# Layer 2's finishing of a graph network: the projection issued in pieces, layer norm in steps out of PSUM, and two more PSUM slots

## The chip, the cores and the metric

The kernel runs on one core of one Trainium2 chip. The metric is device time in microseconds (us). The core's engines each have a queue of their own that is worked through in order: PE (TensorE, matmuls), DVE (VectorE), ACT (ScalarE), POOL (GpSimd, which here only issues gathers) and SP (SyncE, which issues the other DMAs). Engines wait for each other through semaphores.

## The reference

```python
def _rgcn_layer(x, src, dst, edge_type, w_rel, root, bias):
    seg = dst * NUM_REL + edge_type
    xs = x[src]
    sums = jax.ops.segment_sum(xs, seg, num_segments=N * NUM_REL)
    cnt = jax.ops.segment_sum(jnp.ones(seg.shape, x.dtype), seg, num_segments=N * NUM_REL)
    mean = (sums / jnp.maximum(cnt, 1.0)[:, None]).reshape(N, NUM_REL, -1)
    return jnp.einsum('nrd,rdo->no', mean, w_rel) + x @ root + bias
...
h = jax.nn.relu(_rgcn_layer(x, src, dst, edge_type, w_rel1, root1, b1))
out = _layernorm(x + _rgcn_layer(h, src, dst, edge_type, w_rel2, root2, b2))
```

There are 12,500 nodes with 128 features, 200,000 edges sorted by destination, and 10 relations. The relation of an edge is the argmax of ten of its attributes. All is float32.

## The kernel before, in words

**Tiles and windows.** Edges are taken 128 at a time (a tile). POOL gathers the 128 source rows of a tile into a slot of `g` (`gathered`, L684; the pool has six buffers of eight slots, so 48 tiles can be gathered ahead). ACT multiplies each row with one over its count (`scaled`, L690). DVE builds a 0/1 matrix `oh` that tells for each edge its relation and its place in a window of w nodes (`ones`, L698 and L701). PE multiplies the two into a PSUM slot `zp` of 10 x w columns (L895 in layer 1, L1217 in layer 2), and DVE adds that to the running sums `cc` in SBUF (`sum_into`, L725). `cc` is a ring of 1,024 nodes for each layer.

**Blocks.** When all edges of a block of 512 nodes are in `cc`, the block is finished: `projected` multiplies the ten relations' sums with their weights (ten matmuls into one PSUM tile `pf`, L673) and adds one last matmul (L675), and the block's part of the ring is cleared on ACT (`cleared`, L656). Layer 1 also computes that part of layer 2's sums whose sources are known already, projects it (`second`, L808) and stores it transposed in DRAM as `T2`, bias and root term included.

**Layer 2** (`layer_2`, L1103) takes the tiles of which layer 1 could do nothing (166) and the edges left over, which `brought_together` and `listed` compress into 799 tiles. The fewer edges a row keeps, the wider is the window of a tile: w goes from 14 up to 46, in bunches of three tiles, then two, and from w = 26 on one tile to a bunch. The last 115 tiles have w = 46, which is 460 columns. The order of the instructions is written out by hand. For bunch p it records: `ones` for bunch p + 3; the gathers, scalings and matmuls of bunch p; `sum_into` of bunch p - 2; then the steps of a finished block that are due. `zp` has three PSUM buffers (`ps_y`, L952). The table that `ones` compares with is kept in the first 480 columns of a PSUM tile of three banks, `mask` (name "go", L958 and L1029 to L1031); its other two banks are only used while the list is made.

**Finishing in layer 2** (`finish`, L1153). A class `Later` holds steps with a due time, counted in tiles i. At i all eleven matmuls of the projection are recorded in one go, the last of them an identity matmul that adds the stored part `fT` (from `T2`). Then: `turn` at i + 6 (ACT copies `pf` to SBUF as `a`, L1164; PE transposes it, L1167), clearing at i + 8 and i + 12, and `norm` at i + 10 (`normed`, L627: DVE adds x from `xb`, L634; takes the moments, L637 and L638; ACT takes the square root, L640; DVE the reciprocal, L641, and four scalings, L644). Where the ring is about to be written again, `free_until(k)` is a latest time `by` for turning and clearing. With 128-node blocks at the end, layer 2 has 26 blocks, k = 0 to 25.

Of the kernel before, what the change touches and what calls it, by code (L numbers as in the profile page):

```python
# [9 lines left out]
F32 = mybir.dt.float32  # L10
BF16 = mybir.dt.bfloat16
I32 = mybir.dt.int32
AF = mybir.ActivationFunctionType
ALU = mybir.AluOpType
# [6 lines left out]
P = 128  # L21
NREL = 10
# [18 lines left out]
YB = 512  # L41
RN = 2 * YB
# [13 lines left out]
def rgcn_resnorm_kernel(ctx: ExitStack, tc: tile.TileContext, x, src, dst, attr, w_rel1, root1, b1,  # L56
# [498 lines left out]
    def block(k):  # L555
        n0 = nodes[-1][k]
        n = (nodes[-1] + [N])[k + 1] - n0
        return n0, n, [(t, min(P, n - t * P)) for t in range(-(-n // P))]
# [14 lines left out]
    def rows_in(k):  # L573

        last = "e" if k == len(nodes[-1]) - 1 else ""
        xb = fin.tile([P, len(block(k)[2]) if last else 4, C], F32, name="xb" + last)
        rows_dma(xb, x, k, False)
        return xb
# [72 lines left out]
    def cleared(l, k, h):  # L651

        n0, n, _ = block(k)
        o = n0 % RN
        H = NREL // 2
        nc.scalar.activation(cc[:, l, h * H:(h + 1) * H, o:o + n], zero[:, None, :n].to_broadcast([P, H, n]), AF.Copy)  # L656
# [6 lines left out]
        nc.vector.tensor_tensor(s, s, e, op=ALU.add)  # L663
        nc.vector.memset(e, 0.0)

    def projected(k, l, last, po=None, more=True):

        n0, n, _ = block(k)
        o = n0 % RN
        if po is None:  # L670
            po = ps_f.tile([P, YB], F32, name="pf")
        for r in range(NREL if more else 0):
            nc.tensor.matmul(po[:, :n], wsb[l][:, r, :], cc[:, l, r, o:o + n], start=(r == 0), stop=False)  # L673
        w, f = last
        nc.tensor.matmul(po[:, :n], w, f[:, :n], start=not more, stop=True)  # L675
        return po

    def stored(hb, b, k):
# [86 lines left out]
    def layer_1():  # L765
# [7 lines left out]
        def finish(k, t):  # L773

            todo.run(END)
            if k not in fTs:
                xbs[k] = rows_in(k)
                fTs[k] = features_in(k, 0, xbs[k])
            u = QB if t < NT else 0
            folded(ALL, k, WN)  # L780
            po = [projected(k, 0, (rsb[0], fTs[k]))]
            both = starts[k + 1] > bounds(T0)[0] if k + 1 < NBLK else True
            reused = starts[k] + RN < N
            assert not reused or t + 7 * u <= (starts[k] + RN - OFF - WN) // STEP

            def rows_out(_):
                a = po.pop()
                a = fin_a.setdefault(k, shifted(a, k, 0))
                pr = ps_f.tile([P, 4, C], F32, name="pf")
                n0, n, subs = block(k)  # L790
                for i, h in subs:
                    nc.tensor.transpose(pr[:h, i, :], a[:, i * P:i * P + h], ident)
                po.append(pr)

            def rows_kept(_):
                pr = po.pop()
                hb = fin.tile([P, 4, C], F32, name="hb")
                for p, s in spans(k):
                    nc.scalar.activation(hb[:p, s], pr[:p, s], AF.Copy)
                rows_dma(hb, hD, k, True)  # L800
                if k <= K1:
                    first = 0 if k <= K0 else (k - K0) % 2
                    stored(hb, first, k)
                    if k < K1:
                        when = t + 8 * QB if k < K0 else first_seen[k] + 2 * QB
                        todo_late.append((when, lambda t: stored(hb, 1 - first, k)))

            def second(_):  # L808
                po.append(projected(k, 1, (rsb[1], fin_a.pop(k)), more=both))

            def second_kept(_):
                n0, n, _ = block(k)
                p2 = po.pop()
                t2 = fin.tile([P, YB], F32, name="v")
                nc.scalar.activation(t2[:, :n], p2[:, :n], AF.Identity, bias=bsb[1])  # L815
                nc.sync.dma_start(T2[:, n0:n0 + n], t2[:, :n])

            todo.at(t + u, rows_out)
            todo.at(t + 2 * u, rows_kept)
            if reused:  # L820
                todo.at(t + 2 * u, lambda t: cleared(0, k, 0))
                todo.at(t + 3 * u, lambda t: cleared(0, k, 1))
            todo.at(t + 3 * u, second)
            todo.at(t + 5 * u, second_kept)
            if both:
                todo.at(t + 6 * u, lambda t: cleared(1, k, 0))
                todo.at(t + 7 * u, lambda t: cleared(1, k, 1))
            if k + 1 < NBLK - 1:
                def fetch(t):
                    xbs[k + 1] = rows_in(k + 1)  # L830

                def turn(t):
                    n0, n, subs = block(k + 1)
                    pt = ps_f.tile([P, YB], F32, name="pf")
                    for i, h in subs:
                        nc.tensor.transpose(pt[:, i * P:i * P + h], xbs[k + 1][:h, i, :], ident[:h, :h])
                    po.append(pt)

                def turned_kept(t):
                    n0, n, subs = block(k + 1)  # L840
                    pt = po.pop()
                    fTs[k + 1] = fin.tile([P, 4 * P], F32, name="fT")
                    nc.scalar.activation(fTs[k + 1][:, :n], pt[:, :n], AF.Copy)
                todo.at(t + u, fetch)
                todo.at(t + 5 * u, turn)
                todo.at(t + 6 * u, turned_kept)
# [256 lines left out]
    def layer_2():  # L1103
# [30 lines left out]
        def free_until(k):  # L1134

            return next((i for i, hi in enumerate(highs) if hi > starts_2[k] + RN), len(order))
# [3 lines left out]

        todo, jobs = Later(), Later()
        done = 0
        xbs, fTs = {}, {}

        def fetched(k):
            if k < NB2 and k not in xbs:
                n0, n, subs = block(k)
                last = "e" if k == len(nodes[-1]) - 1 else ""
                xbs[k] = rows_in(k)
                fTs[k] = fin.tile([P, (len(subs) if last else 4) * P], F32, name="fT" + last)  # L1150
                nc.sync.dma_start(fTs[k][:, :n], T2[:, n0:n0 + n])

        def finish(k, i):  # L1153

            todo.run(END)
            fetched(k)
            u = 1 if i < len(order) else 0
            folded(TWO, k, WZ)
            n = block(k)[1]
            po = [projected(k, 1, (ident, fTs[k]))]  # L1160

            def turn(_):
                a = fin.tile([P, YB], F32, name="a")
                nc.scalar.activation(a[:, :n], po.pop()[:, :n], AF.Copy)  # L1164
                pr = ps_f.tile([P, 4, C], F32, name="pf")
                for b, h in block(k)[2]:
                    nc.tensor.transpose(pr[:h, b, :], a[:, b * P:b * P + h], ident)  # L1167
                po.append(pr)

            def norm(_):  # L1170
                normed(k, xbs[k], po.pop())
                if k + 1 < NB2 - 1:
                    fetched(k + 1)

            reused = starts_2[k] + RN < N
            by = free_until(k) if reused else END
            assert i < by
            todo.at(min(i + 6 * u, by), turn)
            if reused:
                todo.at(min(i + 8 * u, by), lambda i: cleared(1, k, 0))  # L1180
                todo.at(min(i + 12 * u, by), lambda i: cleared(1, k, 1))
            todo.at(i + 10 * u, norm)

        fetched(0)
        flag = None
# [2 lines left out]
        i = 0  # L1188
        jobs.job(0, brought_together(), QB)
        NB = len(bunches)  # L1190
        made = 0
        for p in range(-AH, NB + BE):
            if p + AH < NB:
# [7 lines left out]
            if p < NB:  # L1201
                second, t0, n, w = bunches[p]
                oh = ohs.pop(p)
                zp = zps[p] = ps_y.tile([P, YB], F32, name="zp")
                for j in range(n):
                    if made % GQ == 0:
                        g = gpool.tile([P, GQ * C], F32, name="g")
                    gs[p, j] = g, made % GQ
                    made += 1
                    idx = (idxB if second else idxE)[:, t0 + j:t0 + j + 1]  # L1210
                    gathered(g, gs[p, j][1], hD, idx, 1)
                for j in range(n):
                    scaled(*gs[p, j], (wB if second else wE)[:, t0 + j:t0 + j + 1])
                m = NREL * w
                for j in reversed(range(n)):
                    gt, b = gs.pop((p, j))
                    nc.tensor.matmul(zp[:, j * m:(j + 1) * m], gt[:, b * C:(b + 1) * C], oh[:, j * m:(j + 1) * m],  # L1217
                                     start=True, stop=True)
                i += n
# [199 lines left out]
```

## Time and profile before

| what | value |
|---|---|
| runs shown | 3320.06, 3318.46, 3319.7 us; median 3319.7 us |
| profiled execution, its own time | 3311.85 us |
| its span in the trace | 3309.8 us |
| busy: PE, DVE, ACT, POOL | 71%, 59%, 50%, 73% |
| gathers issued: layer 1, layer 2 | 166 + 1397, 166 + 799 |
| first and last gather of layer 2 start at | 1982.0 and 3208.2 us of the span |
| layer 2's last projection starts at | 3294.15 us |

An engine's busy share is an average over stages with different limits. In most of the span POOL issues one gather after the other; the last hundred microseconds have no gather any more. So the questions to the profile are how long POOL sets the pace, and what works on after its last gather.

### The profile page before, as it was taken

How to read it: one execution, taken by the hardware profiler on the slowest of the kernel's cores; microseconds unless marked ns; L12 is line 12 of the kernel's file. 1: busy time of each engine (PE TensorE's matmuls, PEld its weight loads, DVE VectorE, ACT ScalarE, POOL GpSimd, SP SyncE). 2: the span in 40 equal slices, each digit the busy share in tenths (PEclk: the TensorE clock that was granted, in tenths of full speed). 3: DMA queues.
4: the chain of work that ended last, by engine and by line, in shares of the span. 5: the costliest groups of instructions: out<-in, count | busy, mean ns of one | idle time of the engine just before them, and what ended most of it. 6: DMA issues, size and time to landing. Idle time of an engine off the chain costs nothing. (4 is left out here: it accounts for less than half of the span.)

```text
span 3309.8 us, 38851 instructions
## 1 busy us (share of the span) xinstructions
PE 2335.7 (71%) x10229; PEld 1650.2 (50%) x10229; DVE 1962.0 (59%) x4847; ACT 1670.3 (50%) x4283; POOL 2404.7 (73%) x2542
## 2 busy tenths in 40 slices
PE   3657777777778777777777871455656677778887
PEld 2445555555556555555655571344444445433333
DVE  7655656565646565555555543977644546567775
ACT  4336666666666666666666663134333434434232
POOL 7777777777777777777777757777777777777750
PEclk7769899988888898888898995567656667799998
DMA  7675444545444545454544332122222222222220
GB/s 229 184 204 178 132 150 131 158 124 157 127 153 128 154 128 158 122 159 120 155 117 123 113 113 66 50 71 78 64 62 63 72 62 72 62 73 81 72 61 28
DMA packets 257039, 376.78 MB, mean 114 GB/s; under 512 B 50066, under 2 KB 181315, under 8 KB 256812
## 3 DMA queue, kind: packets, MB, share of 16 engines
q0 software_dynamic: 103248, 257.39, 27.1%
q1 hardware_dynamic: 99763, 91.19, 8.7%
q10 hardware_dynamic: 53801, 25.62, 2.7%
q8 instruction: 87, 1.43, 0.2%
q14 instruction: 140, 1.15, 0.1%
HBM read 330.41 MB, written 56.39 MB: 117 GB/s over the span
## 5 line engine op out<-in xcount | busy, mean ns | idle before, releaser
L684 POOL DMA_INDIRECT g<-XH,idxE x1397 | 1321.1, 946 | 431.6 <-issue 405.7
L725 DVE TENSOR_TENSOR cc<-cc,zp 128x240 f32 (+15 forms) x2528 | 978.2, 387 | 1094.3 <-PE zp L895 542.7
L895 PE MATMUL zp<-oh,g 128*128 128x120 f32 x5920 | 911.4, 318 | 487.7 <-ACT g L690 389.9
L895 PEld LDWEIGHTS zp<-oh,g 128*128 128x128 f32 x5920 | 851.6, 227 | 584.2 <-ACT g L690 474.3
L684 POOL DMA_INDIRECT g<-hD,idxB x799 | 756.6, 947 | 244.4 <-issue 218.8
L690 ACT ACTIVATE g<-g,wE 128x128 f32<-128x128 f32 x1729 | 665.3, 394 | 510.5 <-DMA g<-XH,idxE 319.5
L1217 PE MATMUL zp<-oh,g 128*128 128x120 f32 (+16 forms) x1930 | 617.6, 472 | 422.5 <-ACT g L690 251.9
L1217 PEld LDWEIGHTS zp<-oh,g 128*128 128x128 f32 x1930 | 409.5, 263 | 624.1 <-ACT g L690 462.1
L673 PE MATMUL pf<-cc,w 128*128 128x512 f32 (+2 forms) x1600 | 665.2, 573 | 10.2 <-DVE cc L663 6.6
L690 ACT ACTIVATE g<-g,seenE 128x128 f32<-128x128 f32 x1397 | 543.8, 389 | 0.0
L690 ACT ACTIVATE g<-g,wB 128x128 f32<-128x128 f32 x799 | 283.6, 394 | 378.5 <-DMA g<-hD,idxB 344.8
L673 PEld LDWEIGHTS pf<-cc,w 128*128 128x128 f32 x1600 | 304.3, 203 | 332.5 <-issue 310.7
L656 ACT ACTIVATE cc<-zero 128x2560 f32<-128x2560 f32 (+2 forms) x144 | 318.3, 2220 | 2.3 <-DVE keyb L1065 1.2
L701 DVE TENSOR_TENSOR oh<-go,keyB 128x460 f32<-128x460 f32 (+11 forms) x481 | 274.0, 570 | 0.0
L698 DVE TENSOR_TENSOR oh<-bank,keyE 128x480 f32<-128x480 f32 x391 | 253.2, 648 | 0.0
L684 POOL DMA_INDIRECT g<-hD,idxE x166 | 166.7, 1004 | 76.3 <-issue 51.8
L684 POOL DMA_INDIRECT g<-in_x_dram,idxE x166 | 156.9, 945 | 51.6 <-issue 45.7
L1164 ACT ACTIVATE a<-pf 128x512 f32<-128x512 f32 (+3 forms) x26 | 14.8, 571 | 275.7 <-PE pf L675 275.7
L606 ACT ACTIVATE a<-pf,b 128x512 f32<-128x512 f32 (+2 forms) x28 | 17.6, 630 | 200.2 <-PE pf L675 200.2
L476 DVE TENSOR_TENSOR eqb<-bank,kh 128x1344 bf16<-128x1344 f32 (+2 forms) x65 | 100.4, 1548 | 0.4
L815 ACT ACTIVATE v<-pf,b 128x512 f32<-128x512 f32 (+2 forms) x28 | 17.7, 632 | 146.9 <-PE pf L675 131.8
L485 PE MATMUL pf<-eqb,identb 128*128 128x512 bf16 (+2 forms) x130 | 55.1, 424 | 10.9 <-DVE eqb L476 10.8
(185 smaller groups left out, 895.4 us busy)
## 6 DMA issues: line engine op xcount, KB each, us to landing
m<-in_edge_attr_dram SPq DMA_DIRECT2D x48, 672.0 KB
g<-XH,idxE POOLq DMA_INDIRECT x1397, 2.8
g<-hD,idxB POOLq DMA_INDIRECT x799, 2.5
XH<-in_x_dram ACTq DMA_DIRECT2D x24, 512.0 KB
XH<-zero ACTq DMA_DIRECT2D x24, 512.0 KB
xb<-in_x_dram SPq DMA_DIRECT2D x46, 256.0 KB
XH<-hb SPq DMA_DIRECT2D x35, 256.0 KB
hD<-hb SPq DMA_DIRECT2D x23, 256.0 KB
```

Source lines behind the costliest of these rows:

```text
L476: nc.vector.tensor_tensor(eq[:p], kpP[:p, None, :R].to_broadcast([p, DB, R]), fore, op=ALU.is_equal)
L485: nc.tensor.matmul(pc[:p], identb[:p, :p], eq[:p, k:k + 4, L:], start=(d + k == 1), stop=False)
L656: nc.scalar.activation(cc[:, l, h * H:(h + 1) * H, o:o + n], zero[:, None, :n].to_broadcast([P, H, n]), AF.Copy)
L673: nc.tensor.matmul(po[:, :n], wsb[l][:, r, :], cc[:, l, r, o:o + n], start=(r == 0), stop=False)
L684: nc.gpsimd.indirect_dma_start(out=g[:, j * C:(j + n) * C], out_offset=None, in_=table, in_offset=bass.IndirectOffsetOnAxis(ap=idx, axis=0))
L690: nc.scalar.activation(s, s, AF.Copy, scale=w)
L698: nc.vector.tensor_tensor(o.rearrange("p (t m) -> p t m", m=m), cols[:, None, :m].to_broadcast([P, n, m]), keys[:, :, None].to_broadcast([ ...
L701: nc.vector.tensor_tensor(o.rearrange("p (t r n) -> p t r n", r=NREL, n=w), cols[:, None, :, :w].to_broadcast([P, n, NREL, w]), keys[:, :, ...
L725: nc.vector.tensor_tensor(s, s, z, op=ALU.add)
L815: nc.scalar.activation(t2[:, :n], p2[:, :n], AF.Identity, bias=bsb[1])
L895: nc.tensor.matmul(zp[:, a + l * KW:a + (l + 1) * KW], g[:, (slot[j] + l) * C:(slot[j] + l + 1) * C], oh[:, j * KW:(j + 1) * KW], start=Tr ...
L1217: nc.tensor.matmul(zp[:, j * m:(j + 1) * m], gt[:, b * C:(b + 1) * C], oh[:, j * m:(j + 1) * m], start=True, stop=True)
```

## The change

It touches both layers. In layer 1, `second` adds x to the stored part: one more identity matmul, with the block's transposed features. In layer 2:

- the x rows are not loaded any more; `fT` alternates between two buffers, and the next block's is asked for when a block begins to finish
- the eleven matmuls are eleven steps, spread over `spread` tiles, where `spread` is at most 10 and at most `by - i - 3`
- `turn` comes at i + spread + 4, clearing at i + spread + 5 and i + spread + 8, none later than `by`
- layer norm reads the transposed block from PSUM, in four steps two tiles apart: `moments` (DVE), `deviation` (ACT), `factors` (DVE), `put` (ACT, four scalings with a bias)
- from the fourth bunch of compressed tiles on, two of every five `zp` slots are the other two banks of `mask`

```diff
-    def projected(k, l, last, po=None, more=True):
+    def projected(k, l, last, more=True):
...
-        w, f = last
-        nc.tensor.matmul(po[:, :n], w, f[:, :n], start=not more, stop=True)
+        for i, (w, f) in enumerate(last):
+            nc.tensor.matmul(po[:, :n], w, f[:, :n], start=not more and i == 0, stop=i == len(last) - 1)
...
-                po.append(projected(k, 1, (rsb[1], fin_a.pop(k)), more=both))
+                po.append(projected(k, 1, [(rsb[1], fin_a.pop(k)), (ident, fTs[k])], more=both))
...
-            po = [projected(k, 1, (ident, fTs[k]))]
+            live = i < len(order)
+            spread = max(0, min(10, by - i - 3)) if live else 0
+            u = 1 if live else 0
+            po = [ps_f.tile([P, YB], F32, name="pf")]
+            some = {}
+
+            def piece(r):
+                w, f = (ident, fTs[k][:, :n]) if r == NREL else (wsb[1][:, r, :], cc[:, 1, r, o:o + n])
+                nc.tensor.matmul(po[0][:, :n], w, f, start=r == 0, stop=r == NREL)
...
-            def norm(_):
-                normed(k, xbs[k], po.pop())
-                if k + 1 < NB2 - 1:
-                    fetched(k + 1)
...
+            def moments(_):
+                mv = some["mv"] = small.tile([P, 4, 2], F32, name="mv")
+                for t, h in subs:
+                    st = small.tile([P, nc.vector.BN_STATS_DIM], F32, name="st")
+                    nc.vector.bn_stats(st[:h], po[0][:h, t, :])
+                    nc.vector.bn_aggr(mv[:h, t, :], st[:h])
+            def deviation(_):
...
+                    nc.scalar.activation(some["rstd"][:p, s], some["mv"][:p, s, 1], AF.Sqrt, bias=eps[:p])
+            def factors(_):
...
+                    nc.vector.reciprocal(some["rstd"][:p, s], some["rstd"][:p, s])
+                    nc.vector.scalar_tensor_tensor(some["back"][:p, s], some["mv"][:p, s, 0], -1.0, some["rstd"][:p, s],
+                                                   op0=ALU.mult, op1=ALU.mult)
+            def put(_):
...
+                    nc.scalar.activation(out_rows[:h, t, :], pr[:h, t, :], AF.Identity, bias=some["back"][:h, t:t + 1],
+                                         scale=some["rstd"][:h, t:t + 1])
+                rows_dma(out_rows, out, k, True)
+            for r in range(NREL + 1):
+                todo.at(i + r * spread // NREL, lambda _, r=r: piece(r))
+            todo.at(i, lambda _: fetched(k + 1))
+            todo.at(min(i + (spread + 4) * u, by), turn)
             if reused:
-                todo.at(min(i + 8 * u, by), lambda i: cleared(1, k, 0))
-                todo.at(min(i + 12 * u, by), lambda i: cleared(1, k, 1))
-            todo.at(i + 10 * u, norm)
+                todo.at(min(i + (spread + 5) * u, by), lambda i: cleared(1, k, 0))
+                todo.at(min(i + (spread + 8) * u, by), lambda i: cleared(1, k, 1))
+            for j, step in enumerate((moments, deviation, factors, put)):
+                todo.at(i + (spread + 6 + 2 * j) * u, step)
...
+        FIRST = sum(not b[0] for b in bunches) + AH
...
-                zp = zps[p] = ps_y.tile([P, YB], F32, name="zp")
+                spare = (p - FIRST) % 5 if second and p >= FIRST else 0
+                if spare < 3:
+                    zp = zps[p] = ps_y.tile([P, YB], F32, name="zp")
+                else:
+                    zp = zps[p] = mask[:, (spare - 2) * YB:(spare - 1) * YB].bitcast(F32)
```

## The prediction, made before the change was run

> **What bounds the kernel now.** I read the stages first, then who waits at the end. POOL's own row for the compressed tiles of layer 2 (engine, op, tile: shortest/median/longest ns, first and last start):
>
> ```profile
> L684 POOL DMA_INDIRECT g<-hD,idxB x799: 940/944/1297, 2208.5 to 3208.2; - x200
> ```
>
> 799 gathers in 1000 us are one per 1.25 us without a break, so up to 3208 POOL sets the pace. But the span goes on to 3309.8: 101.6 us of work are behind. The waits of ACT after 2997 us (engine, line, releaser: us in all, times, longest) tell since when:
>
> ```profile
> ACT a L1164 <- PE pf L675: 141.2, 11, 20.2
> ...
> ACT g L690 <- DMA g<-hD,idxB: 16.4, 18, 1.9
> ```
>
> ACT hardly waits for a gather any more. It stands in front of a projection, 141 of 313 us. So from about 2960 on, tiles are ready before they are used, and the backlog grows. Who is the bound there? DVE's timeline of the block k = 20 (start, duration, work, idle before):
>
> ```profile
> 3173.41 0.62 DVE L725 TENSOR_TENSOR cc<-cc,zp 128x460 f32 x1
> 3173.95 0.63 DVE L701 TENSOR_TENSOR oh<-go,keyB 128x460 f32<-128x460 f32 x1
> 3181.87 0.63 DVE L725 TENSOR_TENSOR cc<-cc,zp 128x460 f32 x1 [7.29 <-PE zp L1217]
> 3182.42 0.63 DVE L701 TENSOR_TENSOR oh<-go,keyB 128x460 f32<-128x460 f32 x1
> 3182.97 0.62 DVE L725 TENSOR_TENSOR cc<-cc,zp 128x460 f32 x1
> ...
> 3190.03 0.68 DVE L634 TENSOR_TENSOR v<-pf,xb 128x512 f32<-128x512 f32 x1
> ...
> 3193.02 1.11 DVE L644 TENSOR_SCALAR o<-v,mv,rstd 128x128 f32<-128x128 f32 x4
> 3194.05 0.62 DVE L701 TENSOR_TENSOR oh<-go,keyB 128x460 f32<-128x460 f32 x1
> 3194.60 0.62 DVE L725 TENSOR_TENSOR cc<-cc,zp 128x460 f32 x1
> ```
>
> and PE's of the same block:
>
> ```profile
> 3171.35 8.85 PE L673 MATMUL pf<-cc,w 128*128 128x512 f32 x20
> 3180.04 1.02 PE L675 MATMUL pf<-fT,ident 128*128 128x512 f32 x2
> 3180.90 4.93 PE L1217 MATMUL zp<-oh,g 128*128 128x460 f32 x12
> ```
>
> A tile costs DVE a `sum_into` and a `ones`, from 3181.87 to 3182.97: 1.09 us. It costs PE two passes, 4.93/12 x 2 = 0.8 us (0.77 between starts). So DVE is the bound, but for the 7.3 to 7.9 us of a projection, and for the norm, 3190.03 to 3194.05 = 4.0 us. Check: 20 x 1.09 + 7.3 + 4.0 + 0.8 (folding) = 33.9, and from this projection to the next, at 3205.08, are 33.7. POOL needs 20 x 1.25 = 25. From the projection at 2959 to the one at 3269 nine blocks (k = 14 to 22: 25, 28, 25, 22, 20, 18, 20, 21, 14 tiles) take 310 us.
>
> **The change, part by part**
>
> *The two spare PSUM slots.* They lie in the tile whose first bank holds the table that `ones` reads. In the order of the changed kernel's built instructions, with what each waits for, the program takes that tile as one. The `ones` after a matmul into a spare slot waits for this matmul, and a matmul into a spare slot waits for the `ones` recorded just before it. In before no `ones` waits for PE. So in two of five bunches DVE and PE go one after the other: `ones` 0.63, then 0.14 until the matmul starts (a sum that ends at 3195.22 lets PE start at 3195.36), then a lone pair of passes 1.04 (PE at 3160.61). That is 1.81 us where DVE needs 1.09, so 1.44 us more for five tiles. At 290 columns (rows: `ones` 0.451, pair 0.76) the step is 1.35 against 0.74, 1.2 more for five. Before 2960 this hides under POOL: with 290 columns five tiles then cost 2 x 1.35 + 3 x 0.74 = 4.9 us, and POOL needs 6.25. Behind it nothing hides it, for DVE is the bound; queued behind the waiting `ones` is every sum. The nine blocks have 193 tiles. In each I take off 8: about six in which PE is the bound anyway (next part), two hidden under the norm's steps. That leaves 121 tiles, 24 groups of five at 1.35: **+33 us**. Bounds: 0, if the order's waits are always over in time, and 193/5 x 1.44 = 56.
>
> The Trainium skill, "PSUM — Partial Sum Buffer", section "PSUM bank collisions raise a hardware error", asks for a guard only between engines in one bank; the table and the spare slots are in different banks. By that rule the chip needs none of these waits, and the sum would lack the 33 us (first rival). They are in the program all the same.
>
> *The projection in pieces.* Same passes: 22 x 0.43 = 9.5 us of PE. The due times give the spread: `by - i - 3` is 4, 9, 7, 5, 1, 1, 4, 5, 4 for k = 14 to 22, so it never reaches 10 here. With a spread of 4, PE does 9.5 us and five tiles (3.9) in a row, 13.4 us, in which DVE wants 5.5 and a tile or two of lead. It loses 13.4 - 6.5 = 7, as now (7.3 to 7.9). Cover would need PE's slack of 1.09 - 0.77 = 0.3 us per tile, some 30 tiles. **-3 us** in all; bounds -10 and +8.
>
> *Norm.* DVE loses the addition and the scalings. It keeps the moments (3190.75 to 3192.44 in before: 1.7 us) and gets `factors`, two operations like L641 (0.18) with a gap, 0.45. So 2.15 for 4.0, nine times: **-17 us**. No row shows the statistics read PSUM; DVE's copies out of PSUM of this size (L1088, 266 ns) take what the statistics take from SBUF (269), so I take no difference. `put` costs ACT four scalings at 0.30 to 0.39, and ACT is idle for two thirds of a block. If its function needed another table, each block would pay two loads like the page's ACT_TABLE_LOAD (1283 ns), 0 to 2.6 us of ACT; only two such loads stand in the whole span, though square root and copy alternate 27 times, so 0.
>
> *Clearing.* Turning and both clears now fall together on `by`, three tiles behind the last piece. ACT copies and clears for 0.6 + 4.55 = 5.1 us and no tile is scaled meanwhile, while PE has three scaled tiles, 3 x 1.3 = 3.9 us. Before, the copy came earlier, and in two blocks DVE lost 1.3. Net about 1 per block: **+8 us** (0 to +18).
>
> *Start of the backlog.* At k = 14 POOL is still close: the first 4 us vanish in its slack: **-4**.
>
> *The rest.* Early in layer 2 POOL waits 2.0, 2.2 and 4.7 us, the last behind a projection of 10.6 us at 2144.3; in pieces, **-2** (0 to -4.7). Layer 1 gets 28 more identity matmuls (L675: 1.02 us for 512 columns, 0.39 for 128) beside a PE that POOL keeps waiting; only those of the last four small blocks stand on the path: **+1**. Of SP's DMAs, the x rows go; nobody waited for them but in the last blocks, where PE waits 3.4 us for `fT`. That wait goes, but the last blocks' chains (pieces, copy, transposes, moments, root, factors, `put`) still run one after the other, and `put` now stands ahead of the last tiles' scaling on ACT: 0 (-4 to +4).
>
> Sum: 33 - 3 - 17 + 8 - 4 - 2 + 1 = **+16**. A second way: I walked through k = 20 instruction by instruction with these durations, from the `ones` of its tile i. Last piece ends at 14.1; `ones` of i + 8 at 17.6 (before 16.7); ACT's clump holds `ones` of i + 10 until 21.6; moments 22.7 to 24.4; the next block's at 36.4, against 33.8 in before: +2.6. Nine such blocks less the 4 are +20. I take **+18**. On the profiled execution's own 3311.85 (span 3309.8 and 2 us around it) that is 3330; it lies 8 below the median of the runs shown, and I count from the median: 3319.7 + 18 = **3338**.
>
> **The rivals**
>
> *The spare slots' waits cost nothing* (0.20). If PE is always far enough ahead, the sum is 16 - 33 = -17 at most. My walk without these waits gives 33.25 for k = 20, -0.5 per block, since ACT's clump then shows in full: -5, with the -2 some **3312**. It decides if five tiles of 460 columns still take 5.45 us.
>
> *The pieces do remove DVE's stall* (0.08, the other side): 7.5 x 9 = 68 us less, **3252**. That needs PE to run the pieces while DVE sums, so a lead of six tiles; it has two, and at spread 1 (k = 18, 19) ten pieces stand in a row as now.
>
> *The clock falls* (0.10). PE's lines in the gather-bound stage:
>
> ```profile
> 2592.65 1.57 PE L1217 MATMUL zp<-oh,g 128*128 128x180 f32 x4 [1.26 <-ACT g L690]
> ...
> 2622.70 1.99 PE L1217 MATMUL zp<-oh,g 128*128 128x180 f32 x12
> 2624.53 0.60 PE L1167 MATMUL pf<-ident,a 128*128 128x128 f32 x4
> 2625.34 0.85 PE L1217 MATMUL zp<-oh,g 128*128 128x180 f32 x4 [0.22 <-DVE cc L725]
> ```
>
> The same four passes take 1.57 us with pauses of about 1 us and 0.85 behind a projection: the granted clock was halved. With more pauses in the backlog stage, the two lone pairs of each group of five could take 1.8 for 1.04: 24 x 1.5 = 36 more, **3374**. Against it: at 290 columns with pauses of 0.5 us (2949 to 2959) the granted clock was 1.00, and there PE streams less (0.5 of 1.25 us) than it would here (3.85 of 6.9). The Trainium skill, "TensorE: Matmul & The Clock Gate", "HAM oscillation", names only pauses over some 3.4 us as harmful; by it this rival has no chance, but the row above has half the clock at pauses of 1.3 us, so it keeps one.
>
> **How the numbers follow.** Forecast 0.60 (3338, own range 3322 to 3356 by the bounds), free waits 0.20, no stall 0.08, clock 0.10, else 0.02. A measurement tells 0.2% (6.6 us) from no change. Free waits lie half in that band; 0.03 of the forecast does too. So faster 0.19, same 0.13, slower 0.68. Range: from the free waits' 3312 less 4 to the forecast's top plus some of the clock: 3308 to 3366.
>
> **What would show it.** Right: `ones` (DVE) with idle time that a zp matmul ends, in two of five bunches; five tiles of 460 columns in about 6.9 us; 36 us from projection to projection at k = 20; last gather still near 3206; DVE busy less. Wrong: such blocks in 30 us or less, POOL's waits longer before 2960, or half-clock pairs.

## The result, and the profile after

The changed kernel takes **3366.4 us** (median of 4 runs, 3365.9 to 3369.9) beside 3319.9 us for the kernel before on the same chip: the ratio is 1.0144, with a 95% interval of 1.0131 to 1.0157. It is 46.6 us slower; the forecast was 18 slower. The profiled execution after is an ordinary one (3366.63 us, span 3364.8), the profiled one of before lies 8 us under its median, so the two profiles differ by 54.8. One of the eight runs of the norm alone (experiment 3) took 3318.4 us at a granted clock of 0.735, where the others had 0.812 to 0.817; its ratio and interval have this run in them.

The gathers' row, and the waits behind 2997 us (engine, line, releaser: us in all, times, longest):

```profile
L683 POOL DMA_INDIRECT g<-hD,idxB x799: 938/944/1300, 2210.2 to 3250.7; - x200
```

```profile
ACT a L1172 <- PE pf L1168: 167.2, 11, 20.0
DVE oh L700 <- PE go L1253: 108.4, 67, 9.2
...
PE go L1253 <- DVE oh L700: 41.7, 37, 4.1
...
POOL g L683 <- PE zp L1253: 23.4, 5, 9.6
```

Second and third line are new: DVE's one-hots wait 67 times for a matmul into a spare slot (`go` is the name of the tile that they lie in), and these matmuls wait 37 times for a one-hot. A gather still takes 944 ns, but the last one starts at 3250.7 instead of 3208.2: POOL now waits for PE, because the ring of gathered tiles is full. That is an effect of the backlog, not its cause.

DVE's timeline of block 20 (start, duration, work, idle before it and its releaser), from the middle of its projection on, whose pieces run from 3207.70 to 3221.91:

```profile
3213.32 0.63 DVE L700 TENSOR_TENSOR oh<-go,keyB 128x460 f32<-128x460 f32 x1
3215.26 0.63 DVE L724 TENSOR_TENSOR cc<-cc,zp 128x460 f32 x1 [1.31 <-PE zp L1253]
3221.09 0.64 DVE L700 TENSOR_TENSOR oh<-go,keyB 128x460 f32<-128x460 f32 x1 [5.20 <-PE go L1253]
3221.65 0.62 DVE L724 TENSOR_TENSOR cc<-cc,zp 128x460 f32 x1
3222.93 0.64 DVE L700 TENSOR_TENSOR oh<-go,keyB 128x460 f32<-128x460 f32 x1 [0.65 <-PE go L1253]
3223.48 0.62 DVE L724 TENSOR_TENSOR cc<-cc,go 128x460 f32 x1
```

and PE's in the same stretch:

```profile
3217.64 0.93 PE L1253 MATMUL zp<-oh,g 128*128 128x460 f32 x2
3218.41 1.88 PE L1168 MATMUL pf<-cc,w 128*128 128x512 f32 x4
3220.12 0.94 PE L1253 MATMUL go<-oh,g 128*128 128x460 f32 x2
3220.89 1.02 PE L1168 MATMUL pf<-fT,ident 128*128 128x512 f32 x2
3221.88 1.01 PE L1253 MATMUL go<-oh,g 128*128 128x460 f32 x2
```

Between 3221.09 and 3222.93 one-hot follows one-hot in 1.84 us, as worked out (1.81), with 0.65 us of idle time. But look at 3215.89 to 3221.09. The `zp` matmul of 3217.64 is over at 3218.57, and its sum could run. It stands in DVE's queue behind a one-hot that waits 5.20 us for the `go` matmul of 3220.12, and that matmul stands behind pieces. In before, DVE's stall at this place ended with a sum. From block 20's projection to the next one's it is 40.3 us, where the forecast walked through this block to 36.4 and before took 33.7.

Where the time went, from the starts of PE's projections (first piece) in each profile. The columns are the start of block 14's projection, from there to block 23's (nine blocks, 193 tiles), and from there to the end of the span. The rows below the line are the experiments.

| kernel | block 14 at | nine blocks | to the end |
|---|---|---|---|
| before | 2959.3 | 310.0 | 40.5 |
| after | 2965.9 | 357.7 | 41.2 |
| --- | | | |
| slots alone | 2974.8 | 370.0 | 41.9 |
| slots, but not next to a projection | 2971.3 | 352.3 | 41.8 |
| after, three slots | 2955.9 | 301.6 | 44.6 |
| after, five slots without waits | 2963.9 | 307.2 | 44.5 |
| five slots without waits, one piece | 2967.0 | 293.5 | 35.9 |
| norm alone | 2960.7 | 291.0 | 35.3 |
| three slots, one piece | 2959.7 | 288.5 | 33.6 |
| three slots, one piece, late due times | 2961.9 | 293.2 | 37.3 |

So 47.7 of the 55 us came in the nine blocks of the backlog. Differences of some 5 us in the first column mean little: the first projection of layer 2, before any spare slot is used, starts anywhere from 2143.8 to 2152.4 in these runs. Each row is one execution, and these lie up to 8 us from their kernel's median (the one of three slots with one piece 5.6 under it).

### The profile page after: what moved, and what is told of

The parts are those of the page before. It is cut to its first block, busy times and chain, and to the rows that moved or that the text cites. A ratio compares the mean times of both kernels' runs of the same rounds, so it can differ in the third digit from the quotient of the medians.

```text
span 3364.8 us, 38665 instructions
## 1 busy us (share of the span) xinstructions
PE 2383.4 (71%) x10285; PEld 1688.7 (50%) x10285; DVE 1930.0 (57%) x4749; ACT 1707.8 (51%) x4381; POOL 2402.3 (71%) x2542
## 5 line engine op out<-in xcount | busy, mean ns | idle before, releaser
L724 DVE TENSOR_TENSOR cc<-cc,zp 128x240 f32 (+13 forms) x2212 | 850.4, 384 | 803.3 <-PE zp L894 563.3
L894 PE MATMUL zp<-oh,g 128*128 128x120 f32 x5920 | 920.9, 320 | 458.1 <-ACT g L689 359.5
L894 PEld LDWEIGHTS zp<-oh,g 128*128 128x128 f32 x5920 | 863.3, 230 | 551.4 <-ACT g L689 442.9
L1253 PE MATMUL zp<-oh,g 128*128 128x120 f32 (+16 forms) x1298 | 418.4, 477 | 282.7 <-ACT g L689 150.1
L1253 PEld LDWEIGHTS zp<-oh,g 128*128 128x128 f32 x1298 | 294.8, 276 | 418.7 <-ACT g L689 301.1
L672 PE MATMUL pf<-cc,w 128*128 128x512 f32 (+2 forms) x1080 | 431.0, 555 | 2.1 <-DVE cc L663 1.7
L1253 PE MATMUL go<-oh,g 128*128 128x150 f32 (+15 forms) x632 | 237.4, 507 | 172.2 <-ACT g L689 101.5
L1253 PEld LDWEIGHTS go<-oh,g 128*128 128x128 f32 x632 | 136.0, 257 | 277.4 <-ACT g L689 183.7
L1168 PE MATMUL pf<-cc,w 128*128 128x512 f32 (+3 forms) x520 | 249.7, 610 | 13.5 <-DVE cc L663 9.4
```

What stands on the lines that cost most here:

```text
L724: nc.vector.tensor_tensor(s, s, z, op=ALU.add)
L894: nc.tensor.matmul(zp[:, a + l * KW:a + (l + 1) * KW], g[:, (slot[j] + l) * C:(slot[j] + l + 1) * C], oh[:, j * KW:(j + 1) * KW], start=Tr ...
L1168: nc.tensor.matmul(po[0][:, :n], w, f, start=r == 0, stop=r == NREL)
```

## The experiments

Each was timed beside the kernel before on the same chip; its median was 3314 to 3317 there, so ratios are given. Of the theories, **S** puts the loss into the spare slots' waits, **R** a good part of it into pieces, clears and `put`.

**1. The change without its spare slots.**

```diff
-                spare = (p - FIRST) % 5 if second and p >= FIRST else 0
+                spare = 0
```

> The changed kernel with three PSUM slots for all bunches as in before, so that no one-hot (ones) waits for a matmul; the pieces, the norm's steps and the clearing times stay. Theory S (nearly all of the loss is the spare slots' waits, and they cost more than the forecast's 33 us because the lone pairs of passes that they leave run at half clock): the forecast's other terms add up to -17, so about 3303, with the span of the last nine blocks' projections 17 below before's, and lone pairs of 460 columns back near 1.04 us. Theory R (the waits cost the 33 us that they were priced at, and the remaining 30 us of the measured +47 come from the rest: the projection in pieces in front of DVE's one-hots, the copy and both clears in a row on ACT, and put's four scalings ahead of the tiles' scaling): about 3333, slower than before with the slots gone.

3304.6 us, ratio 0.9968 (0.9956 to 0.9980): faster than before. With the slots gone, so is the loss: by the ratios 58 us lie between this kernel and the change (62 by the medians, which come from different chips). That is theory S in the time. Its reason, half the clock in the lone pairs, holds for a part only: behind 2960 us, 17 of the 67 lone pairs of 460 columns in after took over 1.3 us. And the nine blocks are only 8.4 us shorter than before's, not 17.

**2. The spare slots alone, put into the kernel before.**

```diff
...
-                zp = zps[p] = ps_y.tile([P, YB], F32, name="zp")
+                spare = (p - FIRST) % 5 if second and p >= FIRST else 0
+                if spare < 3:
+                    zp = zps[p] = ps_y.tile([P, YB], F32, name="zp")
+                else:
+                    zp = zps[p] = mask[:, (spare - 2) * YB:(spare - 1) * YB].bitcast(F32)
```

> The kernel before with the two spare slots and nothing else of the change. Theory S: the waits alone cost 47 + 17 = 64 us or near it, so 3375 to 3385, with two lone pairs in five bunches at 1.6 us or more behind 2960. Theory R: the forecast's 33 us, 3350 to 3356.

3386.3, ratio 1.0207 (1.0194 to 1.0221), +70 us. Theory S's time again, from the other side: the slots cost about twice their forecast with or without the rest of the change. Again most lone pairs are not slow: 12 of 61 took over 1.3 us.

**3. The norm alone.** Three slots, the projection in one piece, turning and clears at the times of before, the norm's steps 8 to 14 tiles behind.

```diff
-            spread = max(0, min(10, by - i - 3)) if live else 0
+            spread = 0
...
-            todo.at(min(i + (spread + 4) * u, by), turn)
+            todo.at(min(i + 6 * u, by), turn)
...
-                todo.at(min(i + (spread + 5) * u, by), lambda i: cleared(1, k, 0))
-                todo.at(min(i + (spread + 8) * u, by), lambda i: cleared(1, k, 1))
+                todo.at(min(i + 8 * u, by), lambda i: cleared(1, k, 0))
+                todo.at(min(i + 12 * u, by), lambda i: cleared(1, k, 1))
...
-                todo.at(i + (spread + 6 + 2 * j) * u, step)
+                todo.at(i + (8 + 2 * j) * u, step)
...
```

> The kernel before with the norm from PSUM in steps and x within the stored partial result, three slots, the projection in one piece, turning and clears at before's due times (6, 8 and 12 tiles behind), the steps 8, 10, 12 and 14 behind. Both theories: DVE has 2.15 us of work for a norm instead of 4.0, so 1.85 x 9 = 17 us less, 3300 to 3306. If it comes out near before, DVE's work in the norm isn't what sets the end of these blocks; then put on ACT or the wait for the chain of steps takes back what DVE saves. The difference to the kernel with three slots and pieces is the price of the pieces with their due times: near 0 by S, about 30 us by R.

3292.7, ratio 0.9945 (0.9927 to 0.9963), some 18 us by the ratio and 23 by the medians; the time lies below the 3300 to 3306 expected. The nine blocks take 19.0 us less, where 17 were worked out from DVE's work. The difference to experiment 1, the price of the pieces with their due times, is 12 us, neither near 0 (S) nor about 30 (R).

**4. The table of the one-hots in SBUF.**

```diff
-        tables[WZ] = widest
+        tables[WZ] = wide
```

> The changed kernel with all five slots, but ones reads its table from SBUF (the tile from which it was copied), so that the PSUM tile of the spare slots holds nothing that DVE compares with: five slots in use, no wait between one-hot and matmul. Theory S: the same as three slots without waits or a little below, 3295 to 3305, if a one-hot of 460 columns still takes 0.63 us; each 0.1 us more per one-hot costs some 0.1 x 193 tiles = 19 us behind 2960. Theory R: 3325 to 3335, and what it lies below the kernel with three slots is what two more slots are worth.

3339.9, ratio 1.0068 (1.0055 to 1.0081). Outside both theories, in the main for a reason that has nothing to do with either. A one-hot of 460 columns takes no longer (630 ns for 627), and none waits for PE. But look at POOL's gathers from 2230 to 3000 us (x count, busy us, mean ns, idle before), in this kernel and in that of experiment 1:

```profile
L683 POOL DMA_INDIRECT g<-hD,idxB x598 | 588.7, 984 | 182.2 <-issue 166.7 <-DMA g<-hD,idxB 6.4 <-ACT g L689 3.0
```

```profile
L683 POOL DMA_INDIRECT g<-hD,idxB x617 | 583.1, 945 | 188.0 <-issue 174.9 <-PE zp L1253 4.3 <-ACT g L689 3.7
```

984 ns instead of 945 in the stage where POOL is the bound: some 39 ns x 600 = 23 of the 35 us by which it lies above experiment 1. The rest stays unexplained; 10 of it lie in the nine blocks (311.8 us). The Trainium skill, "SBUF — State Buffer", section "Who interferes with whom", states that a DVE instruction with two SBUF inputs contends with a GpSimd instruction that reads SBUF. Here the one-hot has both inputs in SBUF once its table is there, and the trace agrees (984 ns for 945). As a test of the slots the run is spoilt; the table has to stay in PSUM.

**5. Where a slot's wait costs.** The slots alone, but for the bunches of the eight tiles behind each projection, which the forecast had taken for free:

```diff
...
-                spare = (p - FIRST) % 5 if second and p >= FIRST else 0
+                clear = second and p >= FIRST and i >= since + 8
+                spare = turn_ % 5 if clear else 0
+                turn_ += clear
...
```

> The kernel before with the spare slots, as in the run of the slots alone (3386, +70 on before), but for the bunches of the first eight tiles behind every projection, which take the three ordinary slots. Behind 2918 us 58 bunches instead of 91 use a spare slot. Theory H (the forecast's step: those tiles' waits were hidden behind the projection and the norm and cost nothing): no change, 3380 to 3390. Theory U (nothing is hidden, each spare slot costs the same wherever it lies): 70 x 58/91 = 45 above before, 3358 to 3364. Theory L (the waits next to the projection are the dear ones, since a one-hot that waits for a matmul behind the projection also holds the sums and one-hots behind it, so that PE comes out of the projection with nothing in stock): below 3350.

3365.9, ratio 1.0155 (1.0138 to 1.0172), +52. Not H, and not L; U, a little above it. In the nine blocks 48 bunches use a spare slot instead of 78, and these blocks take 42.3 us more than before instead of 60.0. So the 30 bunches next to a projection had cost 17.6 us, 0.59 each, and the other 48 cost 0.88 each. Why the 30 were not free can be read in DVE's timeline behind block 20's projection, first with the slots everywhere:

```profile
3241.34 0.63 DVE L725 TENSOR_TENSOR cc<-cc,zp 128x460 f32 x1 [7.29 <-PE zp L1222]
3241.89 0.63 DVE L701 TENSOR_TENSOR oh<-go,keyB 128x460 f32<-128x460 f32 x1
3242.43 0.62 DVE L725 TENSOR_TENSOR cc<-cc,zp 128x460 f32 x1
3243.71 0.64 DVE L701 TENSOR_TENSOR oh<-go,keyB 128x460 f32<-128x460 f32 x1 [0.65 <-PE go L1222]
3244.26 0.62 DVE L725 TENSOR_TENSOR cc<-cc,zp 128x460 f32 x1
3245.54 0.64 DVE L701 TENSOR_TENSOR oh<-go,keyB 128x460 f32<-128x460 f32 x1 [0.65 <-PE go L1222]
```

then without them in this place:

```profile
3223.63 0.63 DVE L725 TENSOR_TENSOR cc<-cc,zp 128x460 f32 x1 [7.29 <-PE zp L1224]
3224.18 0.63 DVE L701 TENSOR_TENSOR oh<-go,keyB 128x460 f32<-128x460 f32 x1
3224.73 0.62 DVE L725 TENSOR_TENSOR cc<-cc,zp 128x460 f32 x1
3225.27 0.63 DVE L701 TENSOR_TENSOR oh<-go,keyB 128x460 f32<-128x460 f32 x1
3225.81 0.62 DVE L725 TENSOR_TENSOR cc<-cc,zp 128x460 f32 x1
3226.36 0.63 DVE L701 TENSOR_TENSOR oh<-go,keyB 128x460 f32<-128x460 f32 x1
```

In both the first sum comes 7.29 us late, and from there on DVE has, in these lines, no idle time but that of the slots. One sum behind the projection, DVE is the bound again, at 1.09 us a tile; there is no stretch behind it in which PE is.

Why the other 48 cost more than the forecast's 0.72 (1.44 for two slots) can be read in part. In the nine blocks of this kernel DVE waits 41 times for `go`, 34.0 us in all. Most of these waits take 0.57 to 0.67 us, but eight take 1.5. Such a wait, and the pair of passes that it stands for:

```profile
3242.28 0.64 DVE L701 TENSOR_TENSOR oh<-go,keyB 128x460 f32<-128x460 f32 x1 [1.52 <-PE go L1224]
```

```profile
3240.36 1.87 PE L1224 MATMUL go<-oh,g 128*128 128x460 f32 x2 [0.82 <-DVE oh L701]
```

The pair takes 1.87 us instead of 1.01, as it does before all eight; the granted clock from 3240 to 3243 us is 0.50. Eight waits that are 0.87 us longer make 7 of the 42.3 us.

**6. The change with five slots, without the waits.** The mask's three banks are given up when the lists are made and taken again as three tiles.

```diff
...
+                if second and WZ not in tables:
+                    lists.close()
+                    ps_n = fast.enter_context(tc.tile_pool(name="ps_n", bufs=1, space=PSUM))
+                    tab = ps_n.tile([P, YB], F32, name="tab")
...
-                    zp = zps[p] = mask[:, (spare - 2) * YB:(spare - 1) * YB].bitcast(F32)
+                    zp = zps[p] = ps_n.tile([P, YB], F32, name="s%d" % spare)
```

> The changed kernel with its five slots, where the mask's three PSUM banks are given up once the lists are made and taken again as three tiles: the table of the one-hots and two slots. The instructions are those of the changed kernel; only the waits between one-hots and matmuls in the spare slots are gone. Theory S (the waits are the loss): 3298 to 3308, as with three slots (3305). If it stays near 3366, the waits aren't it but something that the spare slots themselves do. Theory F (two more slots give PE the lead with which the pieces cover DVE's stall): below 3290.

3313.9, ratio 0.9992 (0.9983 to 1.0001). The same slots without their waits: 50 us of the change's loss are gone by the ratios, and as many in the nine blocks (357.7 to 307.2). So the waits are the loss, though the time lies above theory S's 3308, and theory F is out. DVE's waits behind 2997 us have no one-hot among them any more:

```profile
DVE cc L724 <- PE zp L1257: 50.1, 31, 8.7
DVE cc L724 <- PE s L1257: 24.1, 19, 3.2
DVE st L1180 <- PE pf L1173: 14.4, 3, 6.3
```

It lies 8 us above three slots by the ratios. In the profiles it is 13.5 us, of which 6.6 stand before the first spare slot is used and 5.5 in the nine blocks; what causes these stays open. The two slots, free of waits, win nothing.

**7. The same five slots with the projection in one piece** (edit of number 6, and `spread = 0`).

> The same five free slots with the projection in one piece at the change's due times; beside it stands the run with three slots, 3289. Theory N (three slots suffice: PE's lead is set by the one-hots and scaled tiles in stock): 3285 to 3293. Theory F (two tiles more of lead, 1.5 us per block in ten blocks): 3270 to 3280.

3293.5, ratio 0.9937 (0.9922 to 0.9952), at the upper end of theory N: no faster than three slots (number 9). More slots were not what the kernel lacked.

**8. Five slots in another way, and what they cost.** Two kernels, the norm alone and the change, with the table in a bank of its own, `ps_y` with five banks, and the mask of the list making in SBUF. Both leave out keeping the 12-wide table: the 48-wide one overwrites it while bunches of layer 2's first 166 tiles still compare with it, so that part of the output is another; instructions and sizes are the same.

```diff
...
-    ps_y = fast.enter_context(tc.tile_pool(name="ps_y", bufs=3, space=PSUM))
+    ps_y = fast.enter_context(tc.tile_pool(name="ps_y", bufs=5, space=PSUM))
...
-    mask = ps_m.tile([P, 3 * YB], I32, name="go")
+    mask = comp.tile([P, ER], I32, name="go")
+    tab = ps_m.tile([P, YB], F32, name="tab")
```

> The norm alone with five real slots: the table of the one-hots has a PSUM bank of its own, the mask of the list making lies in SBUF, and five banks take turns, without any wait between one-hot and matmul. Theory N (PE's lead is set by the three one-hots recorded ahead and by the scaled tiles, not by the slots): 3288 to 3297, as with three slots. Theory F (two more slots let PE run two tiles further before it needs a sum, 2 x 0.77 = 1.5 us less stall in each of ten blocks): 3275 to 3282. The mask in SBUF can make the gathers of the first 2300 us longer, which the times of the early projections show by themselves.

> The changed kernel with five real slots in the same manner (table in its own bank, mask of the list making in SBUF): what the change would be without its waits. Theory N: 3300 to 3308, as with three slots. Theory F: with a lead of five tiles the pieces do cover DVE's stall in part, so that it comes out below the norm alone with five slots; at 7.5 us of stall removed in part in ten blocks, 3250 to 3285.

3323.0 (1.0028, 1.0018 to 1.0037) and 3337.8 (1.0074, 1.0059 to 1.0090). Neither theory gives this. The first one's gathers of layer 2's first part have a mean of 1243 ns from 2000 to 2420 us where the norm alone has 1015, and its last gather starts at 3237.0 instead of 3208.3: the list making, with its mask in SBUF, held POOL up by 29 us. Its nine blocks take 296.3 us, no less than with three slots (291.0); those of the second kernel take 303.3 (301.6).

**9. What the pieces cost.** Three slots, the projection in one piece, at the change's close due times:

```diff
-            spread = max(0, min(10, by - i - 3)) if live else 0
+            spread = 0
```

> The changed kernel with three slots and the projection in one piece, at the change's own due times (turning 4, clears 5 and 8, the norm's steps 6 to 12 tiles behind). Against it stand the norm alone (3293: same projection, turning 6, clears 8 and 12, steps 8 to 14) and three slots with pieces (3305). Theory P (the 12 us between those two are the pieces: they push the copy, both clears and put into one clump, and in the last blocks they trail behind the last tiles): 3290 to 3297, with the time from block 23's projection to the end near the norm alone's 35 us and not near 45, and the first 2290 us some 5 longer than with pieces. Theory C (the closer due times themselves cost it): 3302 to 3307.

3289.2, ratio 0.9927 (0.9912 to 0.9942). Theory P: it is the projection in pieces, with what hangs on it, that costs the 14 us (by the ratios) to experiment 1. PE's waits from 2960 to 3260 us, with pieces, and in one piece:

```profile
PE zp L1253 <- ACT g L689: 35.5, 18, 3.6
```

```profile
PE zp L1253 <- ACT g L689: 12.8, 15, 2.0
```

With pieces PE stands longer in front of tiles that ACT hasn't scaled. That could be the clump of copy and clears that the pieces' due times bring; experiment 11 tells.

**10. Clears on GpSimd** from block 14 on, with pieces and three slots, to break up this clump.

```diff
...
+        part = cc[:, l, h * H:(h + 1) * H, o:o + n]
+        if late:
+            nc.gpsimd.memset(part, 0.0)
+        else:
+            nc.scalar.activation(part, zero[:, None, :n].to_broadcast([P, H, n]), AF.Copy)
...
```

> Three slots and the projection in pieces (3305), but from block 14 on GpSimd clears the ring instead of ACT, two memsets of 128x2560 a block; POOL has no lack of time there, its gathers being far ahead. Theory K (the pieces cost 15 us against the projection in one piece, 3289, because they push turning and both clears onto one due time, so that ACT scales no tile for 5 us; PE's waits for scaled tiles from 2960 to 3260 were 35.5 us with pieces and 12.8 without): 3290 to 3297, with that wait near 15 us. Theory P (the pieces themselves cost it, by standing in front of the tiles on PE and by trailing behind the last tiles): 3302 to 3308. If POOL's memsets are long or hold DVE up, it is above 3308, and the memsets' duration shows it.

3312.9, ratio 0.9990 (0.9981 to 0.9999). The premise that POOL has time to spare was false. A memset takes 2236 ns and waits in POOL's queue for the pieces (40.2 us busy, 27.3 idle), and ACT then waits for gathers:

```profile
ACT g L693 <- DMA g<-hD,idxB: 165.0, 167, 3.7
```

POOL became the bound, and the run tells nothing on the clump.

**11. The clump without the pieces.** Three slots, due times as with pieces, but all pieces issued at once:

```diff
-                todo.at(i + r * spread // NREL, lambda _, r=r: piece(r))
+                todo.at(i, lambda _, r=r: piece(r))
```

> Three slots, the projection in one piece at once, but turning, clears and the norm's steps at the late due times that the pieces give them (behind the spread: from block 14 on turning and both clears together on the last possible tile). It lies between the one-piece kernel with the close due times (3289) and the one with pieces (3305). Theory K (the clump of copy and clears on ACT is what costs): 3300 to 3307. Theory P (the pieces on PE and their trailing in the last blocks cost): 3286 to 3293.

3294.1, ratio 0.9941 (0.9928 to 0.9955), 1 us above theory P's range and 6 below K's. PE's wait for scaled tiles from 2960 to 3260 us is 15.8 us here, with the clump, and 35.5 with pieces: the clump alone doesn't lengthen it. Of the 13.6 us between pieces and one piece (ratios 0.9968 and 0.9927), some 9 are the pieces' own; the remaining 4.6 would be the late due times, but their intervals overlap. Part of the pieces' cost is at the very end. PE's block 23 in one piece:

```profile
3255.01 6.62 PE L1168 MATMUL pf<-cc,w 128*128 128x384 f32 x20
3261.47 0.81 PE L1168 MATMUL pf<-xb,ident 128*128 128x384 f32 x2
```

and the end of the same projection in pieces, which began at 3257.50:

```profile
3270.27 2.20 PE L1168 MATMUL pf<-cc,w 128*128 128x384 f32 x6
3272.31 0.81 PE L1168 MATMUL pf<-xb,ident 128*128 128x384 f32 x2
```

7.3 us after its start against 15.6. Block 24 has to follow it (a block's pieces are finished before the next one's begin), and the last column of the table has 44.6 with pieces against 37.3.

**12. Pieces only where there is room for ten** and the columns are used again, before 2890 us, with three slots:

```diff
-            spread = max(0, min(10, by - i - 3)) if live else 0
+            spread = 10 if reused and by - i - 3 >= 10 else 0
```

> Three slots, the projection in pieces (spread 10) only for the blocks with room for it and whose columns are used again, all before 2890 us, and in one piece from there on, at the change's due times. If the pieces gain where POOL sets the pace (the third projection lies 5.5 us earlier with pieces than without) and lose only behind 2918 us and in the last blocks, this is the one-piece kernel's 3289 less some 5: 3281 to 3287. If the early gain is eaten up by 2918, 3286 to 3292.

3284.8, ratio 0.9911 (0.9896 to 0.9926), the fastest of all, but its interval overlaps with that of one piece everywhere (number 9). In its profile the third projection of layer 2 comes only 1.2 us early (2284.3, and 2285.5 without pieces), but block 13's comes at 2920.4 against 2919.0: what is gained early isn't there any more. The two are 0.9% and 0.7% faster than before.

## Why the prediction was right in its direction and wrong in its size

**The step that failed** is the term of the spare slots, "In each I take off 8: about six in which PE is the bound anyway (next part), two hidden under the norm's steps." The change is the sum of two: the slots, forecast +33, measured 58 (with and without them, by the ratios); the rest, forecast -17, measured -11. So 25 of the miss of 29 us are in the slots and 6 in the rest, less the 2 by which the forecast was taken above its sum of 16.

- The mechanism and the price of an undisturbed step were right: one-hots wait for `go`, mostly 0.65 us, and 1.84 us pass from one to the next for 1.81 worked out. With the slots alone, five tiles take 6.93 us (3260.83 to 3267.76) for 6.9.
- The tiles taken off were not free. The forecast saw PE run 12 passes in a row behind a projection in before and took PE for the bound. It was running ahead of DVE, which needs its 1.09 us a tile from its first sum on. With the slots alone the bunches of the eight tiles behind each projection cost 17.6 us, where the forecast had 0 (experiment 5).
- The other 48 slots cost 42.3 us there, where the forecast had 33. 7 of these come from eight pairs of passes at half the clock (experiment 5).
- The forecast's own upper bound, the same price on all 193 tiles, was 56; between the kernels with and without slots the nine blocks differ by 357.7 - 301.6 = **56.1**. That it fits so well is in part luck: a bunch next to a projection cost less than the 0.72 us of that price and the others more, and of the 56.1 only 50.5 go with the waits alone (experiment 6).
- "Before 2960 this hides under POOL" holds up to block 13 only: from its projection to block 14's are 45.7 us in after and 40.2 without slots, 5 us more.
- The free waits (rival of 0.20, 3312) need a program without them. Such a program took 3313.9; in the change they are there.
- The clock (rival of 0.10) has a part in it. From 2960 to 3100 us the granted clock was 0.94 before, 0.84 after, 0.96 with three slots. The 17 slow lone pairs in after (up to 1.90 us, some 0.8 too much each) are 14 us of PE, where the rival had 24 groups of two pairs and 36 us. How much of it delays the end of the change itself, no run separates. The Trainium skill, "TensorE: Matmul & The Clock Gate", section "A second HAM failure mode: psum-queue depth-cycling", names short idles between groups of matmuls as a cause of a clock that swings between half and full. The trace agrees in that it swings with short pauses; but of the 17 `go` pairs of 460 columns with 0.82 us in front of them eight ran at 0.50 and eight at 1.00.
- **The pieces** were forecast at -3, -10 to +8, and measure about +9, just outside; the rival that they remove DVE's stall is out. With three slots and pieces DVE waits 68.1 us for `zp` behind 2997 us, in 47 parts; before, it was 69.1 in 13. The stall is cut up, not covered, as the forecast had it. What it missed is their end: the tail was put at 0 and costs 7.3 us with three slots (44.6 for 37.3; in the change itself the tail is 0.7 longer than in before).
- **Clearing** was forecast at +8 and measures some 5, if anything (experiment 11).
- **The norm** was forecast at -17 and measures -19 in the nine blocks, 18 to 23 in all. The statistics take 274 ns from PSUM, for 269 from SBUF; there is still one table load for the root in the whole span.
- **Early**, -2: the third projection of layer 2 comes earlier with pieces, but nothing of it is left at block 13.
- "Last gather still near 3206" was wrong (3250.7), since the forecast had not thought of the full ring; it cost nothing by itself.

## What to carry to other kernels

A buffer that is put into the unused part of another tile takes over that tile's waits, as here: look at what else reads the tile, and on which engine, before counting it as a buffer. When a bounding engine gets a new wait, price it on every item unless a timeline shows that this very engine is idle there; a long run of another engine beside it isn't proof that the bound has moved. And a chain that is cut into pieces ends with its last piece: near the end of a kernel, where nothing follows that could use the gaps, it is better kept whole (7.3 us here).

## What the runs showed of the hardware

The place of DVE's operand changes the length of POOL's gathers: from 2230 to 3000 us, with the one-hots' 48-wide table in SBUF, a gather took 984 ns in the mean, and with it in PSUM 945 to 947. The median is the same (945 and 944), but the longest gather took 1785 ns instead of 1252. The one-hot itself, at 460 columns, took 630 and 626 to 629.

The granted clock can fall to half behind short pauses. In experiment 5 PE stood idle for 1.44 and 0.68 us (in front of 3007.18 and 3008.63) in a stretch with a clock of 1.00 (3002.4 to 3009.1), and from 3009.2 to 3012.5 it was 0.50. A pause of a given length doesn't decide it, though: with the slots alone 19 of the 23 `go` pairs of 460 columns with 0.82 us in front of them ran at 1.00 and four at half. Nor do the waits for `go` alone lower the mean: from 2960 to 3100 us it was 0.84 in the change and with the slots alone, but 0.90 with the clears on GpSimd, where nothing waits for `go`, and 1.00 in the one-piece kernel with three slots. What does decide it stays open.
